# Layer 0's softmax totals in 256 columns, one inverse per head and query, spread by transfers between partitions, and a gate by tanh

## The chip, the cores and the metric

The kernel runs on one core of a Trainium2 chip. The metric is the device time of the launch in microseconds. All data are float32.

## The reference, cut to what matters

Two layers run over x of shape (1, 128, 256, 256): S = 128 rows, each with 256 positions and 256 channels. Both are "x + attention(group norm of x)". Layer 0, which the change touches, has 8 heads of 32 channels:

```python
bias = jnp.einsum('nijz,zh->nhij', pair_repr, bias_proj)[:, None]
gate = jax.nn.sigmoid(msa_repr @ gate_proj).reshape(bs, s, r, head, c)
q, k, v = jnp.split(msa_repr @ qkv_proj, 3, axis=-1)
...
sim = jnp.einsum('nsqhc,nskhc->nshqk', q, k) * scale
sim = jax.nn.softmax(sim, axis=-1)
sim = sim + bias
attend = jnp.einsum('nshqk,nskhc->nsqhc', sim, v) * gate
out = attend.reshape(bs, s, r, cm) @ out_proj
```

The bias is added after the softmax. With E = exp(scale q k) unnormalised and z its sum over the keys, the attended values are (E v) / z + bias v, times the gate. Layer 1 is an attention with 4 heads of 64 channels in a band of 16 positions; the change leaves its arithmetic alone.

## The kernel before, in words

First `pair_repr` is projected to the bias tile `bias_sb`, and x is read once for its statistics. Then layer 0 runs over the 128 rows. A row's data lie with channels on the 128 partitions, in two halves: a tile [128, 2, 256] is (channel within the half, half, query). Heads 0 to 3 are in half 0, heads 4 to 7 in half 1; head 4 x half + j has partitions 32j to 32j + 31, which the code calls `strip(j)`.

The order of the instructions of PE (TensorE), ACT (ScalarE) and DVE (VectorE) is the order written in the code: the loop stands in a block `manual_schedule` for these three. For SP (SyncE, the queue of DMAs) and POOL (GpSimd) a scheduler chooses the order. [...]

One step s of the loop "for s in range(S)" works on several rows at once:

- `scores(s, half)` makes the scores of four heads (16 products into four PSUM banks, line 794) and their exponentials `ex` (L807). It gives back a function that issues the fourth of them. The PSUM banks for scores and projections are one ring of five.
- `join_tiles(s, half, j)` adds the two key halves of two heads (L816), which gives `both`.
- `sum_heads(s - 1)` makes on PE the totals `zs` (L840) and the bias part `bv` (L826). In `zs` the stationary tile is 32 columns of ones, so that each total appears on all 32 partitions of its head.
- `divide(s - 1)` copies `zs` to `z` on ACT (L853), makes d = (1 + e) z (L855), where e = exp(-gate), and inverts it (L856).
- `attend(s - 1)` makes `av`, E v, on PE, and then on DVE at = (bv z + av) d (L871, L872, L874).
- `stretch(names, i, s - 1)` makes the projections q and k, or v and g, of a pair of rows two steps ahead, by seven products in place of eight (`Seven`, `two_of_them`), and among its last products the output projection `po` of row s - 1, which reads `at` (L577 is the line of all these products). `po` comes in four parts, each after one of the last products.
- `least(s - 1)` keeps the minimum of z for a check at the end (L861), `normal(s + 4)` transposes and normalises a later row (L539, L775) and starts the load of x two rows on (L357), and `finish(s - 1)` adds the residual (L885), takes statistics for layer 1 (L889), and every second row stores to the DRAM tensor `x1` (L891).

After the loop come the last row, the statistics of layer 1 and layer 1 itself, whose rows are loaded as `yg` (L750). Layer 1 already spreads inverses by DMA: `by_transfer` sends four rows of `rz` to DRAM (`rz_far`, L1162) and reads them back broadcast (`near`, L1166).

Of the kernel before, what the change touches and what calls it, by code (L numbers as in the profile page):

```python
# [9 lines left out]
F32 = mybir.dt.float32  # L10
# [5 lines left out]
P = 128  # L16
# [23 lines left out]
def conv_preact_kernel(  # L40
# [97 lines left out]
    for base, per_row, per_group in ((0, 1, -CG), (CG - 1, -1, CG)):  # L138
        nc.gpsimd.affine_select(
            out=within.rearrange("p (g c) -> p g c", c=CG), in_=within.rearrange("p (g c) -> p g c", c=CG),  # L140
            compare_op=ALU.is_ge, fill=0.0, base=base, pattern=[[per_group, P // CG], [0, CG]],
            channel_multiplier=per_row,
        )

    w_out_t = const.tile([P, 2, C], F32, name="w_out_t")
# [215 lines left out]
    with ExitStack() as early:  # L361
# [10 lines left out]
        def load_weights():  # L372
            w_raw = pr_pool.tile([P, 8, C], F32, tag="pr", name="w_raw")
            nc.gpsimd.dma_start(out=w_raw[:, 6:8, :], in_=out_w.rearrange("(t p) c -> p t c", p=P))
            nc.gpsimd.dma_start(out=w_raw[:, 0:6, :], in_=w_in.rearrange("(t p) c -> p t c", p=P))
            nc.gpsimd.dma_start(out=w_nat[:, 6:8, :], in_=w_out.rearrange("(t p) c -> p t c", p=P))
            nc.gpsimd.dma_start(out=b_raw[0:6], in_=b_in.rearrange("(t p) -> t p", p=P))
            nc.gpsimd.dma_start(
                out=b_raw[6:8].rearrange("h (a r) -> h a r", a=A),
                in_=b_out.rearrange("(a h r) -> h a r", a=A, h=2),  # L380
            )
            for h in range(2):
                cols = slice(h * P, (h + 1) * P)
                for to, t0, t1 in ((out_sb, 6, 8), (w_nat, 0, 6)):
                    nc.gpsimd.tensor_copy(
                        to[:, 0 : t1 - t0, cols].rearrange("p t (a r) -> p t a r", a=A),
                        w_raw[:, t0:t1, :].rearrange("p t (a h r) -> p t h a r", a=A, h=2)[:, :, h],
                    )

        def turn_weights():  # L390
            for o4 in range(2):
# [340 lines left out]
    with ExitStack() as both:  # L732
# [3 lines left out]
        quarters1 = {w: Quarters(st1, w_in_t, n * C, f"1{w}") for n, w in enumerate("qk")}  # L736
        quarters1["o"] = Quarters(st1, w_out_t, 0, "1o")
        big1 = both.enter_context(tc.tile_pool(name="big1", bufs=2))
        ygs = {}
        rz_far = dram.tile([2, 2, 4, R], F32, name="rz_far")  # L740

        def load1(g):
            if g * XG < S and g not in ygs:

                if g % 7 < 2:
                    yg = big.tile([P, XG * (R // B), C // A], F32, tag="xg", name=f"yg{g}")
                    yg = yg.rearrange("p n c -> p (n c)").rearrange("p (s h q) -> p s h q", h=2, q=R)
                else:
                    yg = big1.tile([P, XG, 2, R], F32, tag="yg", name=f"yg{g}", bufs=5)
                nc.sync.dma_start(out=yg, in_=rows(x1, g * XG, XG))  # L750
                ygs[g] = yg

        with ExitStack() as lay0:
# [58 lines left out]
            def join_tiles(s, half, j):  # L812

                if s < S:
                    ex, both = hd[s, half]
                    nc.vector.tensor_tensor(both[:, j : j + 2], ex[:, j : j + 2, 0, :], ex[:, j : j + 2, 1, :], ALU.add)  # L816
# [15 lines left out]
            def sum_heads(s):  # L832
                if s < 0:
                    return
                zs = ps_av.tile([P, 2, R], F32, tag="z", name=f"zs{s}")
                bv0 = ps_av.tile([P, 2, R], F32, tag="bv", name=f"bv{s}")
                for half in range(2):
                    both = hd[s, half][1]
                    for j in range(4):
                        nc.tensor.matmul(  # L840
                            zs[D0 * j : D0 * (j + 1), half, :], lhsT=ones[:, 0:D0], rhs=both[:, j, :],
                            start=True, stop=True,
                        )
                products(bv0, s, lambda h, kt: bias_sb[:, kt, h, :])
                hd[s] = bv0
                return zs

            def divide(s, zs):
                if s < 0:
                    return  # L850
                i, r = divmod(s, 2)
                z = att.tile([P, 2, R], F32, tag="z", name=f"z{s}", bufs=1)
                nc.scalar.activation(z, zs, AF.Identity, accum_out=zsum[:, s : s + 1])  # L853
                d = att.tile([P, 2, R], F32, tag="d", name=f"d{s}", bufs=1)
                nc.vector.scalar_tensor_tensor(d, res["g", i][:, 2 * r : 2 * r + 2, :], 1.0, z, op0=ALU.add, op1=ALU.mult)  # L855
                nc.vector.reciprocal(d, d)  # L856
                hd[s, "z"] = (z, d)

            def least(s, z):
                if s >= 0:  # L860
                    nc.vector.tensor_reduce(zmin[:, s : s + 1], z, axis=AX.XY, op=ALU.min)  # L861

            def attend(s):
                if s < 0:
                    return
                (ex0, _), (ex1, _), bv0 = hd.pop((s, 0)), hd.pop((s, 1)), hd.pop(s)
                av = ps_av.tile([P, 2, R], F32, tag="av", name=f"av{s}")
                products(av, s, lambda h, kt: (ex0, ex1)[h // 4][:, h % 4, kt, :])
                z, d = hd.pop((s, "z"))
                t = att.tile([P, 2, R], F32, tag="t", name=f"t{s}", bufs=1)  # L870
                nc.vector.tensor_tensor(t, bv0, z, ALU.mult)  # L871
                nc.vector.tensor_tensor(t, av, t, ALU.add)  # L872
                at = row.tile([P, 2, R], F32, tag="at", name=f"at{s}", bufs=1)
                nc.vector.tensor_tensor(at, t, d, ALU.mult)  # L874
                st[s]["at"] = at

            def finish(s):
# [35 lines left out]
            with tc.manual_schedule(engines={mybir.EngineType.PE, mybir.EngineType.Activation, mybir.EngineType.DVE}):  # L913
# [7 lines left out]
                sum_rows(1)  # L921
                most1 = Most(st1, stats1, 3, 1)
                for s in range(S):
                    scores(s, 0)()
                    zs = sum_heads(s - 1)
                    join_tiles(s, 0, 0)
                    divide(s - 1, zs)
                    if s % 2 == 0:
                        e = res["g", s // 2]
                        nc.scalar.activation(e, e, AF.Exp, scale=-1.0)  # L930
                    z = hd[s - 1, "z"][0] if s > 0 else None
                    rest = ((0, 2), (1, 0), (1, 2))
                    if s < S - 1:
                        attend(s - 1)
                        last_exp = scores(s, 1)
                        if s == 4:
                            for weights in quarters1.values():
                                weights.sum()
                        stretch(("qk", "vg")[s % 2], s // 2 + 1, s - 1, last_exp)
                        for half, j in rest:  # L940
                            join_tiles(s, half, j)
                        least(s - 1, z)
                        if s >= S - 3:
                            most1.join(s - S + 3)
                        normal(s + 4)
                        if s % 2 == 1:
                            sum_rows((s + 3) // 2)
                        finish(s - 1)
                    else:

                        scores(s, 1)()
                        for half, j in rest:
                            join_tiles(s, half, j)
                        least(s - 1, z)
                        attend(s - 1)
                load1(0)
                load1(1)
                warm = proj_bank("warm")
# [6 lines left out]
                divide(S - 1, sum_heads(S - 1))  # L965
                last_z = hd[S - 1, "z"][0]
                attend(S - 1)
                for s in (S - 2, S - 1):
                    if s == S - 1:
                        keep_on(4)  # L970
                    for _ in one_by_one(out_sb, st[s]["at"], f"po{s}", lambda ps: st[s].update(po=ps), B):
                        pass
                    finish(s)
# [6 lines left out]

        with ExitStack() as lay:
            ps_av = psum(lay, "1", 4, 0)
            row = lay.enter_context(tc.tile_pool(name="row1", bufs=4))
            att = lay.enter_context(tc.tile_pool(name="att1", bufs=2))
            st, hd, outs = {s: {} for s in range(S)}, {}, {}
# [366 lines left out]
    with tc.If(sure < P):  # L1352
        with ExitStack() as lay:
# [69 lines left out]
            def again(layer, s, mean, rstd):  # L1423
# [38 lines left out]
                if layer == 0:  # L1462
                    ps = by_channel(gate_sb, 0, xn, "pg2")
                    e = two.tile([P, 2, R], F32, tag="e2", name="e2")
                    nc.scalar.activation(e, ps, AF.Exp, scale=-1.0)
                    nc.vector.tensor_scalar(e, e, 1.0, None, op0=ALU.add)
                    nc.vector.reciprocal(e, e)
                    nc.vector.tensor_tensor(at, at, e, ALU.mult)
                po = by_channel(out_sb if layer == 0 else w_out_t, 0, at, f"po2_{layer}")
                o = two.tile([P, 2, R], F32, tag="o2", name=f"o2_{layer}")  # L1470
                if layer == 0:
# [61 lines left out]
```

## Time and profile before

| | |
|---|---|
| median of 3 runs | 3150.04 us (3149.86 to 3153.88) |
| profiled execution | 3153.9 us, span 3152.1 us |
| mean granted TensorE clock | 0.993 |
| share of the span on the chain that ended last | PE 91%, DMA 5%, DVE 2%, ACT 1% |
| layer 0, rows | about 206 to 2045 us |
| one row's step in layer 0 | 14.5 us on average |

The span is the time from the first to the last instruction on the core; what the profiled execution took beyond it lies before and after. "Busy" is the time in which an engine has an instruction under way. Matmuls are pipelined, and their ends are modelled, so PE's busy time is an upper reading. PEld is the load of the stationary tile, which runs beside the products. SPq is SP issuing a DMA, not the transfer itself. In a row of the timeline "[0.87 <-ACT ex L807]" is the idle time before the instruction and what ended it.

### The profile page before, as it was taken

To read this page: it belongs to the slowest core of one execution; us is meant where nothing else is said; L and a number is where in the kernel's file an instruction comes from. 1 tells how busy PE (TensorE), PEld (TensorE's weight loads), DVE (VectorE), ACT (ScalarE), POOL (GpSimd) and SP (SyncE) were. 2 spreads that over 40 slices of the span, in tenths; PEclk is the share of its full clock that TensorE was granted. 3 is DMA by queue.
4 is the path that set the end of the run, shared out by engine and by line. 5 is a ranking of instruction groups with operands and counts; after the bars stand their busy time and mean duration, and the time that the engine had idled before them with its cause. 6 is when DMAs were issued, how large, how long until landed. Compare 5 with 4: busy or idle time off the path is not lost.

```text
span 3152.1 us, 128861 instructions
## 1 busy us (share of the span) xinstructions
PE 3075.5 (98%) x57467; PEld 2114.1 (67%) x57467; DVE 2544.5 (81%) x4140; ACT 1870.0 (59%) x4064; POOL 1622.5 (51%) x1651
## 2 busy tenths in 40 slices
PE   6889999999999999999999999999999999999997
PEld 4556666666666666665666666568888888888886
DVE  4669999999999999999999999956666666666665
ACT  4666666666666666666666666645555555555553
POOL 3034444444444444444444544357777777776774
PEclk9989999999999999999999999999999999999999
DMA  9941111111111111111111111114444444444443
GB/s 374 424 121 43 43 43 36 43 36 43 36 39 40 40 40 36 43 36 43 36 42 37 36 43 36 36 35 98 93 103 96 102 96 97 103 99 100 93 99 70
DMA packets 357266, 245.08 MB, mean 78 GB/s; under 512 B 276072, under 2 KB 342112, under 8 KB 350560
## 3 DMA queue, kind: packets, MB, share of 16 engines
q1 hardware_dynamic: 355808, 234.39, 27.3%
q8 instruction: 453, 7.42, 1.0%
q0 software_dynamic: 752, 2.36, 0.2%
q14 instruction: 109, 0.89, 0.1%
q10 hardware_dynamic: 144, 0.00, 0.0%
HBM read 169.09 MB, written 67.62 MB: 75 GB/s over the span
## 4 chain that ended last, share of the span: by engine, by line
PE 91%; DMA 5%; DVE 2%; ACT 1%; issue 0%; POOL 0%; SPq 0%; DVEq 0%; POOLq 0%; ACTq 0%
PE sim L794 8%; PE po L577 7%; PE p1v L1055 7%; PE bv L826 7%; PE av L826 7%; PE p1q L577 6%; PE p1o L577 6%; PE pv L577 6%; PE pq L577 6%; PE p1k L577 6%; PE pk L577 5%; PE pg L577 5%; DMA pr<-in_L_conv_pair_repr_dram 4%; PE zs L840 4%; PE 1sim L1076 3%; PE 1av L1117 3%
## 5 line engine op out<-in xcount | busy, mean ns | idle before, releaser
L807 ACT ACTIVATE ex<-sim 128x512 f32<-128x512 f32 x1024 | 547.6, 605 | 422.2 <-PE sim L794 422.2
L816 DVE TENSOR_TENSOR both<-ex 128x512 f32<-128x512 f32 x512 | 487.8, 991 | 71.2 <-ACT ex L807 71.0
L856 DVE RECIPROCAL d<-d 128x512 f32<-128x512 f32 x128 | 429.2, 3353 | 4.4
L618 POOL TENSOR_TENSOR v<-v,twovg 128x256 f32<-128x256 f32 x64 | 78.3, 1223 | 544.4 <-ACT twovg L637 544.4
L577 PE MATMUL po<-at,out_sb 128*32 128x256 f32 x4096 | 291.5, 380 | 4.1 <-DVE at L874 4.1
L794 PE MATMUL sim<-q,k 32*64 32x256 f32 x8192 | 288.4, 387 | 1.2 <-ACT ex L807 1.2
L826 PE MATMUL bv<-bias_sb,v 128*32 128x256 f32 x4096 | 244.5, 379 | 0.7 <-DVE t L871 0.7
L826 PE MATMUL av<-ex,v 128*32 128x256 f32 x4096 | 244.5, 379 | 0.0
L1086 POOL TENSOR_TENSOR 1p<-1ex,seen 128x768 f32<-128x768 f32 x127 | 231.0, 1819 | 13.9 <-ACT 1ex L1084 13.9
L1055 PE MATMUL p1v<-w_in_t,1xn 128*64 128x128 f32 x4096 | 237.7, 274 | 0.3 <-POOL place L990 0.3
L794 PEld LDWEIGHTS sim<-q,k 32*64 32x64 f32 x8192 | 152.1, 131 | 126.9 <-issue 79.3
L1055 PEld LDWEIGHTS p1v<-w_in_t,1xn 128*64 128x64 f32 x4096 | 222.3, 137 | 21.5 <-PE p1k L577 20.2
L677 ACT ACTIVATE 1q<-p1q,bqk 128x256 f32<-128x256 f32 x192 | 91.1, 474 | 244.1 <-PE p1q L577 244.1
L1186 DVE TENSOR_TENSOR 1at<-1av,1near 128x512 f32<-128x512 f32 x128 | 82.5, 686 | 151.5 <-DMA 1near<-rz_far 129.0
L618 POOL TENSOR_TENSOR q<-q,twoqk 128x256 f32<-128x256 f32 x64 | 52.0, 812 | 292.4 <-ACT twoqk L637 292.4
L826 PEld LDWEIGHTS bv<-bias_sb,v 128*32 128x32 f32 x4096 | 133.2, 110 | 88.7 <-issue 1.1
L826 PEld LDWEIGHTS av<-ex,v 128*32 128x32 f32 x4096 | 133.2, 110 | 87.9 <-issue 0.4
L577 PEld LDWEIGHTS po<-at,out_sb 128*32 128x32 f32 x4096 | 131.0, 110 | 70.9 <-issue 4.5
L1093 POOL TENSOR_TENSOR 1zp<-1p 128x512 f32<-128x512 f32 x127 | 161.9, 1275 | 10.0
L568 POOL TENSOR_TENSOR 1ts<-1xn 128x256 f32<-128x256 f32 x64 | 47.0, 734 | 232.9 <-ACT 1xn L1016 232.9
L775 DVE TENSOR_SCALAR xn<-xt,mean,rstd 128x256 f32<-128x256 f32 x256 | 160.4, 666 | 0.0
L1062 ACT COPY 1v<-p1v 128x512 f32<-128x512 f32 x128 | 75.1, 587 | 135.1 <-PE p1v L1055 131.7
(300 smaller groups left out, 7687.6 us busy)
## 6 DMA issues: line engine op xcount, KB each, us to landing
pr<-in_L_conv_pair_repr_dram SPq DMA_DIRECT2D x32, 1024.0 KB
xs<-in_x_dram SPq DMA_DIRECT2D x16, 2048.0 KB
x<-o SPq DMA_DIRECT2D x64, 512.0 KB
yg<-x SPq DMA_DIRECT2D x64, 512.0 KB
out_dram<-1o SPq DMA_DIRECT2D x256, 128.0 KB
xg<-in_x_dram SPq DMA_DIRECT2D x252, 128.0 KB
1near<-rz_far SPq DMA_DIRECT2D x124, 256.0 KB
rz_far<-1rz SPq DMA_DIRECT2D x124, 4.0 KB
```

The source lines that it names most:

```text
L577: nc.tensor.matmul(out[cols], lhsT=lhsT[:, cols], rhs=rhs, **flags)
L618: nc.gpsimd.tensor_tensor(self.to[:, 0], self.to[:, 0], two, ALU.add)
L775: nc.vector.tensor_scalar(xns[i][:, 2 * r + half, :], xt[:, half, :], mean0[:, half : half + 1], rstd0[:, half : half + 1], op0=ALU.subtra ...
L794: nc.tensor.matmul(sims[j][KB * c : KB * (c + 1), kt, :], lhsT=k[p0 : p0 + D0, 2 * r + half, k0 : k0 + KB], rhs=q[p0 : p0 + D0, 2 * r + ha ...
L807: nc.scalar.activation(ex[:, j], sims[j], AF.Exp, scale=1.0 / math.sqrt(D0))
L816: nc.vector.tensor_tensor(both[:, j : j + 2], ex[:, j : j + 2, 0, :], ex[:, j : j + 2, 1, :], ALU.add)
L826: nc.tensor.matmul(to[D0 * j : D0 * (j + 1), half, :], lhsT=v[:, 2 * r + half, c0 : c0 + D0], rhs=weights(4 * half + j, kt), start=(kt == ...
L840: nc.tensor.matmul(zs[D0 * j : D0 * (j + 1), half, :], lhsT=ones[:, 0:D0], rhs=both[:, j, :], start=True, stop=True,)
L856: nc.vector.reciprocal(d, d)
L1055: nc.tensor.matmul(ps[KB * half : KB * (half + 1), b, :], lhsT=xns[i][:, 2 * r + kt, KB * b : KB * (b + 1)], rhs=w_in_t[:, kt, 2 * C + P * ...
L1086: engine.tensor_tensor(p.rearrange("p j (r c) -> p (j r) c", c=WROW)[:, :, 0 : 2 * WSTEP] .rearrange("p r (t c) -> p r t c", c=WSTEP)[:, : ...
L1093: engine.tensor_tensor(zp, p[:, :, 0:R], p[:, :, R : 2 * R], ALU.add)
```

## The change

In layer 0, each head's total now stands on one partition instead of 32. The stationary tile `place0` has ones in 16 columns, 0 to 15 for half 0 and 16 to 31 for half 1, so the totals of both halves fill one tile [128, 256]: partitions 32j to 32j + 15 hold head j, the next 16 hold head 4 + j. `z` and its inverse `rz` have 256 columns instead of 512. Eight DMAs a row, issued from SP, each copy one partition of `rz` to the 32 partitions of its head and half in `near`. For the last row two products with the tile `spread0` and a copy on ACT do this. The products with `v` are then at = (av near + bv)(1 + tanh(gate/2)), in the new function `gated`; the factor one half of the sigmoid is put into `out_sb`. On ACT the fourth exponential of `scores(s, 0)` comes after the copy of `z`. On DVE the order of a step becomes: first join, inverse, second join, minimum, normalisation of row s + 4, the three operations of `gated`, the two joins of half 1, residual. The pool of the `yg` tiles is opened in layer 1 instead of ahead of layer 0. The code that recomputes a row in another way when a total is out of range gets the factor 2 that undoes the half.

```diff
+    place0 = const.tile([P, 2, B], F32, name="place0")
+    nc.gpsimd.memset(place0, 0.0)
+    for half in range(2):
+        nc.gpsimd.memset(place0[:, half, 16 * half : 16 * (half + 1)], 1.0)
+    spread0 = const.tile([P, 2, P], F32, name="spread0")
+    for half in range(2):
+        nc.gpsimd.tensor_copy(
+            spread0[:, half].rearrange("p (j d) -> p j d", d=D0),
+            ident[:, 16 * half :: B].unsqueeze(2).to_broadcast([P, A, D0]),
...
+                    if t0 == 6:
+                        nc.gpsimd.tensor_scalar(to, raw, 0.5, None, op0=ALU.mult)
...
-                    yg = big1.tile([P, XG, 2, R], F32, tag="yg", name=f"yg{g}", bufs=5)
+                    yg = pools["yg"].tile([P, XG, 2, R], F32, tag="yg", name=f"yg{g}", bufs=5)
...
                         nc.tensor.matmul(
-                            zs[D0 * j : D0 * (j + 1), half, :], lhsT=ones[:, 0:D0], rhs=both[:, j, :],
-                            start=True, stop=True,
+                            zs[strip(j), 0, :], lhsT=place0[:, half, :], rhs=both[:, j, :],
+                            start=(half == 0), stop=(half == 1),
                         )
...
             def divide(s, zs):
...
-                z = att.tile([P, 2, R], F32, tag="z", name=f"z{s}", bufs=1)
-                nc.scalar.activation(z, zs, AF.Identity, accum_out=zsum[:, s : s + 1])
-                d = att.tile([P, 2, R], F32, tag="d", name=f"d{s}", bufs=1)
-                nc.vector.scalar_tensor_tensor(d, res["g", i][:, 2 * r : 2 * r + 2, :], 1.0, z, op0=ALU.add, op1=ALU.mult)
-                nc.vector.reciprocal(d, d)
-                hd[s, "z"] = (z, d)
+                z = att.tile([P, R], F32, tag="z", name=f"z{s}", bufs=1)
+                nc.scalar.activation(z, zs[:, 0, :], AF.Identity, accum_out=zsum[:, s : s + 1])
+                rz = att.tile([P, R], F32, tag="rz", name=f"rz{s}")
+                nc.vector.reciprocal(rz, z)
+                near = att.tile([P, 2, R], F32, tag="near", name=f"near{s}")
+                if s < S - 1:
+                    for j in range(A):
+                        for half in range(2):
+                            p = B * j + 16 * half
+                            nc.sync.dma_start(
+                                out=near[strip(j), half, :],
+                                in_=rz[p : p + 1].unsqueeze(1).to_broadcast([1, B, R]),
+                            )
+                else:
+                    ps = proj_bank(f"near{s}")
+                    for half in range(2):
+                        nc.tensor.matmul(ps[:, half, :], lhsT=spread0[:, half], rhs=rz, start=True, stop=True)
+                    nc.scalar.copy(near, ps)
+                hd[s, "z"] = (z, near)
...
-                z, d = hd.pop((s, "z"))
+                hd[s, "av"] = (av, bv0)
+
+            def gated(s):
...
                 t = att.tile([P, 2, R], F32, tag="t", name=f"t{s}", bufs=1)
-                nc.vector.tensor_tensor(t, bv0, z, ALU.mult)
-                nc.vector.tensor_tensor(t, av, t, ALU.add)
+                nc.vector.tensor_tensor(t, av, near, ALU.mult)
+                nc.vector.tensor_tensor(t, bv0, t, ALU.add)
                 at = row.tile([P, 2, R], F32, tag="at", name=f"at{s}", bufs=1)
-                nc.vector.tensor_tensor(at, t, d, ALU.mult)
+                nc.vector.scalar_tensor_tensor(
+                    at, res["g", i][:, 2 * r : 2 * r + 2, :], 1.0, t, op0=ALU.add, op1=ALU.mult
+                )
...
                 for s in range(S):
-                    scores(s, 0)()
+                    last_exp = scores(s, 0)
                     zs = sum_heads(s - 1)
                     join_tiles(s, 0, 0)
                     divide(s - 1, zs)
+                    last_exp()
                     if s % 2 == 0:
                         e = res["g", s // 2]
-                        nc.scalar.activation(e, e, AF.Exp, scale=-1.0)
...
+                        nc.scalar.activation(e, e, AF.Tanh, scale=0.5)
+                    attend(s - 1)
+                    join_tiles(s, 0, 2)
+                    if s > 0:
+                        least(s - 1, hd[s - 1, "z"][0])
+                    normal(s + 4)
+                    gated(s - 1)
+                    last_exp = scores(s, 1)
                     if s < S - 1:
-                        attend(s - 1)
-                        last_exp = scores(s, 1)
...
                         stretch(("qk", "vg")[s % 2], s // 2 + 1, s - 1, last_exp)
-                        for half, j in rest:
-                            join_tiles(s, half, j)
-                        least(s - 1, z)
+                    else:
+                        last_exp()
+                    for j in (0, 2):
+                        join_tiles(s, 1, j)
+                    if s < S - 1:
...
-                        normal(s + 4)
...
                         finish(s - 1)
-                    else:
-
-                        scores(s, 1)()
-                        for half, j in rest:
-                            join_tiles(s, half, j)
-                        least(s - 1, z)
-                        attend(s - 1)
...
                 attend(S - 1)
+                gated(S - 1)
```

More of the change, by code (lines that the diff above doesn't have):

```diff
@@ L384, in load_weights @@
                 for to, t0, t1 in ((out_sb, 6, 8), (w_nat, 0, 6)):
[L385 to L388, printed above, removed]
+                    to = to[:, 0 : t1 - t0, cols].rearrange("p t (a r) -> p t a r", a=A)
+                    raw = w_raw[:, t0:t1, :].rearrange("p t (a h r) -> p t h a r", a=A, h=2)[:, :, h]
+                    if t0 == 6:
+                        nc.gpsimd.tensor_scalar(to, raw, 0.5, None, op0=ALU.mult)
+                    else:
+                        nc.gpsimd.tensor_copy(to, raw)
         def turn_weights():
@@ L738, in conv_preact_kernel @@
         big1 = both.enter_context(tc.tile_pool(name="big1", bufs=2))
-        ygs = {}
+        ygs, pools = {}, {}
         rz_far = dram.tile([2, 2, 4, R], F32, name="rz_far")
@@ L850, in divide @@
                     return
-                i, r = divmod(s, 2)
-                z = att.tile([P, 2, R], F32, tag="z", name=f"z{s}", bufs=1)
-                nc.scalar.activation(z, zs, AF.Identity, accum_out=zsum[:, s : s + 1])
-                d = att.tile([P, 2, R], F32, tag="d", name=f"d{s}", bufs=1)
-                nc.vector.scalar_tensor_tensor(d, res["g", i][:, 2 * r : 2 * r + 2, :], 1.0, z, op0=ALU.add, op1=ALU.mult)
-                nc.vector.reciprocal(d, d)
-                hd[s, "z"] = (z, d)
+                z = att.tile([P, R], F32, tag="z", name=f"z{s}", bufs=1)
[17 more added lines that the diff above has]
+                hd[s, "z"] = (z, near)
             def least(s, z):
                 if s >= 0:
-                    nc.vector.tensor_reduce(zmin[:, s : s + 1], z, axis=AX.XY, op=ALU.min)
+                    nc.vector.tensor_reduce(zmin[:, s : s + 1], z, axis=AX.X, op=ALU.min)
             def attend(s):
@@ L868, in attend @@
                 products(av, s, lambda h, kt: (ex0, ex1)[h // 4][:, h % 4, kt, :])
-                z, d = hd.pop((s, "z"))
+                hd[s, "av"] = (av, bv0)
+            def gated(s):
+                if s < 0:
+                    return
+                (av, bv0), near = hd.pop((s, "av")), hd.pop((s, "z"))[1]
+                i, r = divmod(s, 2)
                 t = att.tile([P, 2, R], F32, tag="t", name=f"t{s}", bufs=1)
-                nc.vector.tensor_tensor(t, bv0, z, ALU.mult)
-                nc.vector.tensor_tensor(t, av, t, ALU.add)
+                nc.vector.tensor_tensor(t, av, near, ALU.mult)
+                nc.vector.tensor_tensor(t, bv0, t, ALU.add)
                 at = row.tile([P, 2, R], F32, tag="at", name=f"at{s}", bufs=1)
-                nc.vector.tensor_tensor(at, t, d, ALU.mult)
+                nc.vector.scalar_tensor_tensor(
+                    at, res["g", i][:, 2 * r : 2 * r + 2, :], 1.0, t, op0=ALU.add, op1=ALU.mult
+                )
                 st[s]["at"] = at
@@ L927, in conv_preact_kernel @@
                     divide(s - 1, zs)
+                    last_exp()
                     if s % 2 == 0:
                         e = res["g", s // 2]
-                        nc.scalar.activation(e, e, AF.Exp, scale=-1.0)
-                    z = hd[s - 1, "z"][0] if s > 0 else None
-                    rest = ((0, 2), (1, 0), (1, 2))
+                        nc.scalar.activation(e, e, AF.Tanh, scale=0.5)
[6 more added lines that the diff above has]
+                    last_exp = scores(s, 1)
                     if s < S - 1:
-                        attend(s - 1)
-                        last_exp = scores(s, 1)
                         if s == 4:
@@ L939, in conv_preact_kernel @@
                         stretch(("qk", "vg")[s % 2], s // 2 + 1, s - 1, last_exp)
-                        for half, j in rest:
-                            join_tiles(s, half, j)
-                        least(s - 1, z)
+                    else:
+                        last_exp()
+                    for j in (0, 2):
+                        join_tiles(s, 1, j)
+                    if s < S - 1:
                         if s >= S - 3:
                             most1.join(s - S + 3)
-                        normal(s + 4)
                         if s % 2 == 1:
@@ L982, in conv_preact_kernel @@
             ps_av = psum(lay, "1", 4, 0)
+            pools["yg"] = lay.enter_context(tc.tile_pool(name="yg1", bufs=1))
             row = lay.enter_context(tc.tile_pool(name="row1", bufs=4))
@@ L1467, in again @@
                     nc.vector.reciprocal(e, e)
-                    nc.vector.tensor_tensor(at, at, e, ALU.mult)
+                    nc.vector.scalar_tensor_tensor(at, at, 2.0, e, op0=ALU.mult, op1=ALU.mult)
                 po = by_channel(out_sb if layer == 0 else w_out_t, 0, at, f"po2_{layer}")
```

## The prediction

> **What bounds the kernel now.** I first took the busy shares of the page, then the table of busy time by stretch, then who waited for whom on PE.
>
> ```profile
> PE 3075.5 (98%) x57467; PEld 2114.1 (67%) x57467; DVE 2544.5 (81%) x4140; ACT 1870.0 (59%) x4064; POOL 1622.5 (51%) x1651
> ```
>
> In the stretch from 300 to 1900 us, which is layer 0 in its steady state, PE has no gap at all. The columns are length, then busy time (count) of PE, PEld, DVE, ACT and POOL, then the clock, the DMA share and GB/s:
>
> ```profile
> 300.00:1900.00 1600.00, 1600.00 (x34916) 977.48 (x34912) 1500.56 (x1771) 1033.91 (x2156) 727.29 (x664) 1.00 0.15 40
> PE po L577 <- DVE at L874: 4.1, 2, 3.6
> ```
>
> The second line is PE's wait for `at`, the tile that the change recomputes: 4.1 us in two instances over the span. So DVE, 94% busy there, is not waited for, and time freed on it is worth almost nothing. What counts is whether the new path to `at` is longer than PE can hide.
>
> One row's step, from the timeline (start, length, engine, line, operation). I call 1013.99, the first scores of the row, T. The next row's scores start at 1028.45, so a step is 14.46 us.
>
> ```profile
> 1013.99 1.12 PE L794 MATMUL sim<-q,k 32*64 32x256 f32 x32
> 1015.04 1.07 PE L840 MATMUL zs<-both,ones 128*32 128x256 f32 x16
> 1025.10 0.35 PEld L577 LDWEIGHTS po<-at,out_sb 128*32 128x32 f32 x8
> 1015.17 2.07 ACT L807 ACTIVATE ex<-sim 128x512 f32<-128x512 f32 x4 [1.32 <-PE sim L794]
> 1017.09 0.63 ACT L853 ACTIVATE z<-zs 128x512 f32<-128x512 f32 x1
> 1024.27 0.37 ACT L611 COPY midq<-pq 128x256 f32<-128x256 f32 x1
> 1016.29 1.06 DVE L816 TENSOR_TENSOR both<-ex 128x512 f32<-128x512 f32 x1 [0.87 <-ACT ex L807]
> 1017.91 1.13 DVE L855 SCALAR_TENSOR_TENSOR d<-g,z 128x512 f32<-128x512 f32 x1 [0.56 <-ACT z L853]
> 1019.07 3.35 DVE L856 RECIPROCAL d<-d 128x512 f32<-128x512 f32 x1
> 1022.34 0.63 DVE L871 TENSOR_TENSOR t<-bv,z 128x512 f32<-128x512 f32 x1
> 1023.79 0.69 DVE L874 TENSOR_TENSOR at<-t,d 128x512 f32<-128x512 f32 x1
> ```
>
> PE needs `at` at T+11.1 (1025.10); it has it at T+10.5 (1024.48). The margin is 0.6 us, and everything after `at` on PE, 3.4 us of the step, stands behind that load.
>
> For transfers I looked at SyncE's issues, in layer 0 (first row) and in layer 1, where a similar spreading exists:
>
> ```profile
> 1042.99 1.90 SPq L357 DMA_DIRECT2D xg<-in_x_dram  x4
> 2316.04 1.09 SPq L1162 DMA_DIRECT2D rz_far<-1rz  x2
> 2317.67 1.12 SPq L1166 DMA_DIRECT2D 1near<-rz_far  x2
> ```
>
> One issue occupies SP for about 0.53 us whether it moves 4 KB or 128 KB (1.09/2; the four take 0.31 and then three times 0.53). SP was free again at 2317.13 and waited for the first `rz_far` to land before 2317.67, so a small transfer lands about 1.6 us after its issue starts.
>
> [...] The trace has tables loaded only at layer borders; tanh itself it does not show.
>
> **The change, part by part**, per row unless said.
>
> *PE.* The eight `zs` products keep shape and count, only their target shrinks: 0. *ACT.* `z` is 256 wide instead of 512: 0.37 instead of 0.63. The fourth exp of the first half moves behind `z`; its bank is wanted again by the first projection, at T+6.5, so 0. The gate's tanh takes the place of an exp of 1.06 us: 0. If each gate did switch tables, that would be up to 2 x 1.28 us (the load at 2052.88) every second row on ACT, which is 65% busy; I take 0.
>
> *DVE.* Gone: `d` (909 ns mean), half of the reciprocal (1.68), half of the minimum (about 0.3), together 2.9 us. No time is gained, as PE does not wait for DVE. Least and the normalisation of row s+4 (0.76 + 1.3) move ahead of the gate, under the transfer. The latter has its input two rows early.
>
> *SP.* New: eight issues for each of 127 rows. Behind them in the queue stand, every second row, the four `xg` loads, 4 us later than now but needed two rows on: 0. Ahead of them stands the store of two rows of `x`, which waits for the residual at about T+0.7 to 2.2, issues in 0.40 us, and is off the DMA engines some 3 us after that (the table of 0.75 us slices shows no bytes by then). `near` starts later: 0.
>
> *The path to `at`* is the price:
> - three exps from T+1.2, so `z` starts at T+2.6; 0.37 for it, 0.2 until DVE may read it (now 0.82 from its start to L855's, for 0.63): T+3.2;
> - the reciprocal, behind the first join (done by T+3.0 to 3.4), 1.68: T+4.9;
> - eight issues: the last starts 0.35 + 6 x 0.53 later, T+8.45;
> - landing, 1.6 for a small one: T+10.05;
> - each transfer reads one partition's 1 KB 32 times[...]: T+11.25;
> - [...]three operations, 0.73 + 0.73 (start to start now) + 0.9 (two SBUF inputs, as `d`): `at` at T+13.7.
>
> PE wants it at T+11.1: **2.6 us of idle PE** in each of the 126 steps that hold a `po`. DVE has finished the normalisation by T+8.6 and stands waiting; behind it are the joins of the second half (2 us), done by T+15.7, before the next `zs` at T+18.1. Nothing else becomes late. 126 x 2.6 = 328 us.
>
> *Border.* In the last step the joins of the second half now stand behind row 126's gate. PE resumed `zs` at 2049.72, 9.0 us after that row's scores; now about T+15.7, 6.7 later. The last row's own path is shorter (reciprocal 1.68 less, `d` gone, a product and a copy added): about 2.5 back. Net +4. The `yg` buffers that move to layer 1 are first read after its first stretch: 0. GpSimd's set-up lies in the first 200 us, where it is busy for 35: 0.
>
> Sum against the profiled execution (3153.9 us, span 3152.1): 3153.9 + 328 + 4 = 3486; it was 0.12% above the median of 3150.0, so 3482 for the median.
>
> **The rivals.**
> - [...]Reads of one partition run as fast as others, `near` lands at T+10.05, `at` at T+12.5, idle 1.4 us: 126 x 1.4 + 4 = 180, so 3330. [...]Against: `xg`, into 32 partitions, moves at 156 to 203 GB/s while the store from 128 moved at 350.
> - *Transfers one behind another.* [...]landing at T+15.9, `at` at T+18.3, idle 7.2: 3150 + 910 + 4 = 4064. In-between values are possible.
> - *Hidden, no slower.* If the eighth lands by T+8.6, where DVE ends the normalisation, `at` is there at T+11.0 and PE never waits. It takes issues of at most 0.32 us[...]: 3154, no change. The first issue after a pause takes 0.31, but those behind it 0.48 and a gap.
> - *Faster.* PE would have to be waiting for DVE now; 4.1 us at most is there to be won.
>
> **How the numbers follow.** A 2.6 us stall (2.0 to 3.3): 0.42. [...]: 0.28. Queued transfers (3.3 to 7.3): 0.20. Hidden: 0.07. Faster: 0.03. The likeliest gives 3482. The range 3290 to 3780 runs from a stall of 1.1 to 5.0 us, leaving out the hidden and faster cases and half of the queued one. Some 0.2% (6 us) is what a measurement can tell from no change; of the hidden case part would lie above it: faster 0.03, same 0.05, slower 0.92.
>
> **What would show it.** In the changed profile: `po` waiting for `at` some 126 times at 1 to 3 us; PE's share in layer 0 at about 85%; DVE waiting for DMA `near` before the product of `av`; eight SP issues of about 0.5 us directly after the reciprocal; a step of about 17 us. A step of 14.5 us would refute all of it; a wait at `z`, the fourth exp or `zs` instead of `po` would show a path that I costed at nothing.

## The result, and the profile after

The changed kernel takes 3829.52 us (median of 4 runs, 3818.09 to 3837.51) against 3150.76 us: 1.2145 times the time before, with an interval of 1.2124 to 1.2166. The direction was forecast, the size was not: 679 us were lost where the prediction had 332, and the time lies above the stated range. The profiled execution has a span of 3829.2 us.

First the page's busy times (same columns as before), and the layer 0 stretch of the table of busy time, which was 1.00 in PE's clock column and 0.15 in DMA share before:

```profile
PE 3259.5 (85%) x57471; PEld 2227.2 (58%) x57471; DVE 2017.7 (53%) x4012; ACT 1836.2 (48%) x4065; POOL 1487.2 (39%) x1656
```

```profile
300.00:2000.00 1700.00, 1366.95 (x26985) 836.98 (x26981) 804.49 (x1280) 777.90 (x1668) 467.69 (x514) 0.93 0.31 42
```

DVE lost 527 us of work, as intended. PE now stands still for a fifth of layer 0, and yet its busy time over the span rose by 184 us with the same products: its clock was at 0.93 on average there. The two tables of waits (total, times, longest) say for what PE and DVE waited:

```profile
PE po L590 <- DVE at L905: 487.0, 126, 8.2
PE zs L853 <- DVE both L829: 8.7, 1, 8.7
DVE t L902 <- DMA near<-rz: 494.2, 86, 7.9
DVE t L902 <- DMA xg<-in_x_dram: 252.0, 41, 7.1
```

The first line was 4.1 us in 2 instances before; now each of the 126 steps has its wait. The two DVE lines are one wait, 127 times for `near`: `xg` stands in 41 rows only because it was the last transfer to land there; the gate doesn't read it.

One row in the timeline, beginning with the first scores; T is now 1010.48:

```profile
1010.48 1.12 PE L807 MATMUL sim<-q,k 32*64 32x256 f32 x32
1013.11 0.40 ACT L865 ACTIVATE z<-zs 128x256 f32<-128x256 f32 x1
1013.63 1.75 DVE L867 RECIPROCAL rz<-z 128x256 f32<-128x256 f32 x1 [0.16 <-ACT z L865]
1015.41 5.57 SPq L873 DMA_DIRECT2D near<-rz  x8
1016.85 0.70 DVE L788 TENSOR_SCALAR xn<-xt,mean,rstd 128x256 f32<-128x256 f32 x2
1023.36 0.69 DVE L902 TENSOR_TENSOR t<-av,near 128x512 f32<-128x512 f32 x1 [5.81 <-DMA xg<-in_x_dram]
1024.88 0.69 DVE L905 SCALAR_TENSOR_TENSOR at<-g,t 128x512 f32<-128x512 f32 x1
1025.72 0.71 PE L590 MATMUL po<-at,out_sb 128*32 128x256 f32 x8 [3.70 <-DVE at L905]
1026.15 1.13 PE L590 MATMUL pg<-ts,sums_g 128*32 128x256 f32 x8
1026.98 1.16 PE L590 MATMUL pv<-qkv_sb,ts 128*32 128x128 f32 x16
1027.83 1.16 PE L590 MATMUL po<-at,out_sb 128*32 128x256 f32 x8
1030.57 1.12 PE L807 MATMUL sim<-q,k 32*64 32x256 f32 x32
```

The path is the predicted one: reciprocal done at T+4.9, eight issues on SP, DVE idle from 1017.55 to 1023.36, `at` at T+15.1, PE idle for 3.70 us. The new thing stands behind it. The groups at 1026.15, 1026.98, 1027.83 begin 0.83 to 0.85 us apart. In the kernel before they did so 0.43 us apart:

```profile
1025.32 0.61 PE L577 MATMUL po<-at,out_sb 128*32 128x256 f32 x8
1025.75 0.61 PE L577 MATMUL pk<-ts,sums_k 128*32 128x256 f32 x8
```

After this stall PE runs at half rate: its granted clock is 0.50 from 1026.17 to 1029.58, 3.41 us.

Over rows 3 to 124 of both traces, a step has gone from 14.48 to 19.81 us: 4.0 us more between the product ahead of `po` and `po`, and 1.33 us more from `po` to the scores of the next row's second half (9.97 instead of 8.64). 126 x 5.34 = 673, and 7.3 more at the border's `zs`: 680, against 677 between the two spans.

### The profile page after: what moved, and what is told of

It is laid out like the page before. It is cut to its first block, busy times and chain, and to the rows that moved or that the text cites. A ratio compares the mean times of both kernels' runs of the same rounds, so it can differ in the third digit from the quotient of the medians.

```text
span 3829.2 us, 130233 instructions
## 1 busy us (share of the span) xinstructions
PE 3259.5 (85%) x57471; PEld 2227.2 (58%) x57471; DVE 2017.7 (53%) x4012; ACT 1836.2 (48%) x4065; POOL 1487.2 (39%) x1656
## 3 DMA queue, kind: packets, MB, share of 16 engines
q0 software_dynamic: 752, 2.36, 0.2%
## 4 chain that ended last, share of the span: by engine, by line
PE 50%; DVE 16%; SPq 15%; DMA 13%; issue 3%; ACT 2%; POOL 0%; DVEq 0%; ACTq 0%; POOLq 0%
SPq L873 15%; PE po L590 8%; DMA near<-rz 7%; PE p1v L1088 6%; DVE rz L867 6%; PE p1q L590 5%; PE p1o L590 5%; PE p1k L590 5%; PE sim L807 4%; PE zs L853 3%; PE 1sim L1109 2%; DVE at L905 2%; DMA pr<-in_L_conv_pair_repr_dram 2%; DVE t L903 2%; DVE t L902 2%
## 5 line engine op out<-in xcount | busy, mean ns | idle before, releaser
L590 PE MATMUL po<-at,out_sb 128*32 128x256 f32 x4096 | 385.4, 468 | 487.0 <-DVE at L905 487.0
L590 PEld LDWEIGHTS po<-at,out_sb 128*32 128x32 f32 x4096 | 180.7, 135 | 602.0 <-issue 577.6
L902 DVE TENSOR_TENSOR t<-av,near 128x512 f32<-128x512 f32 x128 | 88.4, 691 | 750.3 <-DMA near<-rz 494.2
L829 DVE TENSOR_TENSOR both<-ex 128x512 f32<-128x512 f32 x512 | 362.7, 729 | 120.4 <-ACT ex L820 118.9
L918 DVE TENSOR_TENSOR o<-po,xt 128x512 f32<-128x512 f32 x128 | 88.6, 692 | 442.5 <-PE po L590 442.5
L631 POOL TENSOR_TENSOR v<-v,twovg 128x256 f32<-128x256 f32 x64 | 46.8, 731 | 567.9 <-ACT twovg L650 567.9
L634 POOL TENSOR_TENSOR v<-v,midv 128x512 f32<-128x512 f32 x64 | 81.6, 1274 | 416.9 <-ACT v L628 416.9
L634 POOL TENSOR_TENSOR q<-q,midq 128x512 f32<-128x512 f32 x64 | 81.6, 1275 | 401.7 <-ACT q L628 401.7
L867 DVE RECIPROCAL rz<-z 128x256 f32<-128x256 f32 x128 | 223.8, 1748 | 13.7 <-ACT z L865 13.2
L626 ACT COPY midg<-pg 128x256 f32<-128x256 f32 x64 | 23.8, 373 | 309.3 <-PE pg L590 309.3
```

The source lines that it names most:

```text
L590: nc.tensor.matmul(out[cols], lhsT=lhsT[:, cols], rhs=rhs, **flags)
L634: nc.gpsimd.tensor_tensor(self.to[:, 2:4], self.to[:, 2:4], self.mid, ALU.add)
L867: nc.vector.reciprocal(rz, z)
L902: nc.vector.tensor_tensor(t, av, near, ALU.mult)
```

## The experiments

Each was timed beside the kernel before on the same chip: e1 to e4 on one, e5 to e8 on a second, e9 on a third. On these three the kernel before took 3150.8, 3150.8 and 3150.3 us. The table gives, from each profile, the mean time from the reciprocal's end to DVE's product of `av` and `near`, PE's whole wait for `at`, and the step.

| kernel | us | reciprocal to `near` in use, us | PE waits for `at`, us | step, us |
|---|---|---|---|---|
| before | 3150.8 | none | 4.1 | 14.48 |
| changed | 3829.5 | 7.99 | 487.0 | 19.81 |
| e1, 32 source partitions | 3665.3 | 7.35 | 397.6 | 18.49 |
| e2, `near` of the row before | 3155.1 | not waited for | 5.6 | 14.48 |
| e3, filler of 4 | 3673.8 | 7.97 | 217.5 | 18.55 |
| e8, filler of 7 | 3641.8 | 7.98 | 54.6 | 18.29 |
| e4, by product | 3289.7 | no transfer | 3.4 | 15.54 |
| e5, four transfers | 3363.5 | 5.66 | 176.8 | 16.09 |
| e6, through DRAM | 3467.9 | 6.12 | 243.1 | 16.94 |
| e7, two queues | 3460.7 | 6.32 | 141.0 | 16.90 |
| e9, two queues, other order | 3384.4 | 5.66 | 66.8 | 16.30 |

**Is the wait all of it? e2.**

```diff
-                near = att.tile([P, 2, R], F32, tag="near", name=f"near{s}")
+                near = att.tile([P, 2, R], F32, tag="near", name=f"near{s}", bufs=3)
...
+                nears[s] = near
+                near = nears[s - 1] if 0 < s < S - 1 else near
```

> The changed kernel, but the gate of a row multiplies with the near of the row before, which landed a step ago: every transfer is still made, none is waited for in its own step. It leaves out the right inverse for rows 1 to 126. Theory that the wait for near is the whole loss: PE waits for at no more, a step of 14.5 us, 3155 to 3160 us (the border costs up to 7). Rival, that the new order, the tanh, the smaller tiles or the DMA traffic cost something of themselves: a step above 14.5 us, 3200 us or more.

Measured: 3155.07 us, ratio 1.0012 (1.0005 to 1.0019). From its page and its waits:

```profile
PE 3075.1 (97%) x57471; PEld 2113.2 (67%) x57471; DVE 1985.3 (63%) x4012; ACT 1841.1 (58%) x4065; POOL 1497.1 (47%) x1656
PE po L590 <- DVE at L907: 5.6, 2, 4.2
```

All transfers are made, the order, the tanh and the smaller tiles are in, and the step is back at 14.48 us. So none of them costs anything that shows: the loss is the wait, with what it does to PE. It also shows what the relief of DVE is worth here. DVE has 559 us less to do than in the kernel before, and nothing is won.

**Why is PE slow after the wait? e3 and e8.** Products of no use go into the bank that `po` then overwrites, ahead of its first part:

```diff
+        for _ in range(fill):
+            nc.tensor.matmul(ps[:, 0, :], lhsT=ident, rhs=out_sb[:, 0, :], start=True, stop=True)
```

> The changed kernel, with four products of no use (1.7 us of PE) ahead of the first part of po, into the bank that po then overwrites. Theory that PE's clock falls to half[...]: the idle stretch shrinks from 4.0 to 2.3 us, the products after it run at full rate (8.64 us from po to the next half's scores instead of 9.97), and 126 x 1.33 = 168 us are won although PE does more: 3660 us. Rival, that PE is slow there for another reason (operands, PSUM, power): the products stay slow, 3830 us; if the filler delays po: up to 4040 us.

> As the filler of four products, with seven (3.0 us): PE's idle stretch is about 1.0 us. Theory that the filler only keeps the clock up and the wait stays: the rest of the slow products goes (8.93 to 8.64 us after po), 126 x 0.29 = 37 us less than with four: 3640 us. Rival, that the filler itself delays po: more than with four, 3700 us or above.

Measured: 3673.75 us with four, 3641.82 us with seven (ratios 1.1651, 1.1598 to 1.1703, and 1.156, 1.1541 to 1.158). Work was added and 156 and 188 us were won. The layer 0 stretch, e3 and then e8 (PE's clock is the third figure from the end):

```profile
300.00:2000.00 1700.00, 1542.64 (x29512) 942.78 (x29508) 847.40 (x1369) 831.65 (x1777) 506.77 (x550) 0.98 0.33 45
```

```profile
300.00:2000.00 1700.00, 1662.31 (x30651) 1054.31 (x30647) 857.19 (x1394) 848.97 (x1812) 517.53 (x560) 1.00 0.34 46
```

The clock goes from 0.93 through 0.98 to 1.00, and the time from `po` to the next half's scores from 9.97 through 8.93 to 8.67 us (8.64 before). The step of e8 is 3.8 us longer than before, about the bare wait.

In the changed kernel, between 300 and 2000 us, the granted clock falls to half 68 times, 65 times for 3.41 us and three times for 6.83, and all these stretches begin on one grid of 3.41 us. What tells a wait with slow products after it from one without is how its idle time lies in the windows of this grid. Here are the wait of the row before the one above, and windows of the grid around the two waits (PE's busy time is the second figure):

```profile
1007.33 0.64 PE L590 MATMUL po<-at,out_sb 128*32 128x256 f32 x8 [3.57 <-DVE at L905]
1002.27:1005.69 3.42, 1.48 (x28) 0.65 (x20) 0.65 (x1) 1.29 (x4) 1.42 (x2) 1.00 0.32 26
1005.69:1009.10 3.41, 1.77 (x36) 1.30 (x40) 2.62 (x5) 0.59 (x2) 0.00 (x0) 1.00 0.00 0
1022.75:1026.17 3.42, 0.45 (x9) 0.36 (x13) 2.67 (x5) 0.00 (x0) 0.00 (x0) 1.00 0.78 140
1026.17:1029.58 3.41, 3.41 (x45) 2.48 (x41) 0.61 (x2) 0.96 (x2) 0.74 (x1) 0.50 0.02 5
```

The wait of 3.57 us falls into two windows, with PE idle for 1.94 and 1.64 us, and nothing slow follows. The wait of 3.70 us has 2.97 us in one window, and the next window is at half clock. Each of the 68 stretches follows a window in which PE was idle for 2.11 us or more, and no such window at full clock goes without (idle by the trace's modelled ends); of the windows at full clock that were followed by full clock, the longest idle one had 2.07 us. In the three stretches of 6.83 us the second half follows a window at half clock with 0.90 to 1.12 us of idle PE. So a wait may or may not cost clock: of the changed kernel's waits for `at`, half clock was granted within the next 3.41 us after 13 of the 26 below 3.5 us (2.88 the shortest), 48 of the 62 from 3.5 to 4 us, and all 38 above.

**What makes the wait 8 us long? e1 and e5.** In e1 only the source is another. The first of the two forecasts below is that of the single source partition being the limit:

```diff
-                                in_=rz[p : p + 1].unsqueeze(1).to_broadcast([1, B, R]),
+                                in_=rz[strip(j)],
```

> The changed kernel, but each of the eight transfers reads the 32 partitions of its strip, 1 KB each, instead of one partition 32 times: the same number of issues and bytes[...]. It leaves out the right placing (half of the channels get the inverse of another head). [...]1 KB packets take well under 100 ns instead of about 240, an issue 0.53 us instead of 0.67, the last landing comes 1.6 us after its issue instead of 3.3; at lies at about T+12.4, PE idles 1.4 us a step[...]: about 3330 us. Issue theory (SP's issue and landing cost what they cost for a transfer of this size, whatever the source): 3830 us, as the changed kernel.

Measured: 3665.32 us, ratio 1.1634 (1.1614 to 1.1653). Neither forecast had it right. SP's queue and the layer 0 stretch of e1:

```profile
970.24 5.32 SPq L873 DMA_DIRECT2D near<-rz  x8
```

```profile
300.00:2000.00 1700.00, 1408.39 (x28756) 865.26 (x28748) 849.90 (x1365) 830.01 (x1777) 503.07 (x550) 0.96 0.18 45
```

With about as many bytes a microsecond, the DMA engines are busy 0.18 of the time instead of 0.31: a packet of 1 KB takes 62 ns on average instead of 239. So the first forecast is right that the source holds the packets. Whether it is the one source partition, or the same 1 KB being read 32 times, e1 doesn't tell, as it changes both. But the issues stayed where they were, 4.82 us from the reciprocal to the start of the last, 4.71 in the changed kernel. The source only sets how long after the last issue `near` is there: 3.0 us in the changed kernel, 2.1 in e1 (rows with no transfer of 16 KB in flight behind the last issue, see the end).

In e5 four transfers are left out:

```diff
-                        for half in range(2):
...
+                            in_=rz[B * j : B * j + 1].unsqueeze(1).to_broadcast([1, B, R]),
...
+                near = near[:, 0:1, :].to_broadcast([P, 2, R]) if s < S - 1 else near
```

> The changed kernel with four transfers a row instead of eight: half 0's only, and the gate uses them for both halves (left out: the inverses of heads 4 to 7 in rows 0 to 126). Theory that the number of issues, about 0.66 us each, sets the landing: the last issue starts 1.9 us after the reciprocal instead of 4.7, at lies at T+12.2, PE idles about 1.1 us a step, its clock stays up: about 3295 us. Rival, [...]the same here, so this run only measures the price of an issue: 2.7 to 2.8 us less stall for four of them, and 1.3 us less for the clock.

Measured: 3363.45 us, ratio 1.0671 (1.0654 to 1.0689). The last issue starts at 1.97 us, as expected, but `near` is in use 3.7 us after it and not 3.0. The packets took 304 ns instead of 239. The four sources, partitions 0, 32, 64 and 96, follow each other without the others in between, and order matters in e9 below; that this is the reason here was not shown. Four issues fewer give 2.3 us.

**Can the path be shortened? e6, e7, e9.** In e6 the rows go through DRAM, in e7 half of the transfers are issued by ACT, and e9 changes the order of e7's transfers alone:

```diff
+                    far = rz_far0[s % 2]
+                    nc.sync.dma_start(out=far, in_=rz.rearrange("(n c) q -> n c q", c=16)[:, 0, :])
+                    for j in range(A):
+                        nc.sync.dma_start(
+                            out=near[strip(j)].rearrange("p h q -> p (h q)"),
+                            in_=far[2 * j : 2 * j + 2].rearrange("n q -> (n q)").partition_broadcast(B),
...
```

```diff
+                    def send(half, queue):
...
+                            queue.dma_start(
...
+                    send(0, nc.sync)
+                    hd[s, "send"] = lambda: send(1, nc.scalar)
...
+                    if s > 0:
+                        hd.pop((s - 1, "send"))()
                     attend(s - 1)
```

```diff
-                        for j in range(A):
+                        for j in ((0, 2, 1, 3), (2, 0, 3, 1))[half]:
```

> The changed kernel, but the inverse goes through DRAM, as layer 1's does: one write of eight rows, then four broadcast reads, five issues in place of eight and no single-partition source. Theory of issues: write landed 2.1 us after the reciprocal, the last read issued 1.6 to 1.9 us later, landed 2.6 us after that: near 6.5 us after the reciprocal instead of 8.0, PE idles about 2.4 us, no clock loss: 3460 us. Rival, that the second hop costs as much as the three issues saved: 8 us again, 3830 us.

> The changed kernel with half 1's four transfers issued from ACT's queue, behind the tanh, half 0's from SP. Theory that SP's issuing is the limit: both queues have issued by 2.0 us after the reciprocal, landing at 5.1, at T+12.3, idle 1.2 us: 3310 us, plus up to 60 us where ACT's exponentials come 0.8 us late. Rival, [...]landing at 7.0, idle 2.9 us: 3530 to 3600 us.

> The kernel with two queues, with the order of the transfers changed alone: SP sends partitions 0, 64, 32, 96, ACT 80, 16, 112, 48 (before: 0, 32, 64, 96 and 16, 48, 80, 112). [...] the last packet ends some 1.0 us sooner after the reciprocal (4.5 instead of 5.5), DVE starts the gate at 5.3 instead of 6.3, PE's wait for at falls from 1.4 to about 0.4 us: 3335 to 3350 us. Rival, [...]no change, 3461 us.

Measured: e6 3467.89 us (1.1012, 1.0986 to 1.1038), e7 3460.74 us (1.098, 1.0962 to 1.0998), e9 3384.41 us (1.0741, 1.0723 to 1.0759). In e6 a second hop is cheaper than three more issues and the slow source: 6.12 us instead of 7.99. In e7 both queues have started their last issue 2.28 us after the reciprocal, and the last packet still ends at 5.49. In e9 the same issues at the same times, in another order, have it end at 4.88 us, with packets of 159 ns instead of 195, and the time falls by 76 us. Only the sequence of the transfers differs between the two, so this shows their order to matter; by what mechanism was not shown. Each transfer has its target strip with its source, so the order of targets changed too. In e1 the targets follow each other as in the changed kernel and the packets take 62 ns, so targets alone don't explain the 239; their part in e9 was not measured apart. The gain is 0.66 us a row, where 1.0 was expected. What ACT's issuing costs stands in PE's waits, e7 and then e9:

```profile
PE po L590 <- DVE at L908: 141.0, 125, 6.6
PE pk L590 <- ACT ex L820: 57.3, 62, 2.0
PE pg L590 <- ACT ex L820: 56.7, 63, 1.8
```

```profile
PE po L590 <- DVE at L908: 66.8, 125, 5.9
PE pg L590 <- ACT ex L820: 57.0, 63, 2.0
PE pk L590 <- ACT ex L820: 56.5, 62, 1.8
```

114 us of new wait, since the exponentials of the second half stand behind the four issues on ACT (2.79 us for the four in e7's row at 1000.18, and the exponentials start at 1003.01).

**Without transfers, e4.**

```diff
+                def by_product():
+                    ps = proj_bank(f"near{s}")
+                    for half in range(2):
+                        nc.tensor.matmul(ps[:, half, :], lhsT=spread0[:, half], rhs=rz, start=True, stop=True)
+                    nc.scalar.copy(near, ps)
...
-                    gated(s - 1)
                     last_exp = scores(s, 1)
+                    if s > 0:
+                        hd[s - 1, "spread"]()
+                    gated(s - 1)
```

> The changed kernel, but every row's inverse is spread by two products with spread0 and a copy on ACT behind the scores of the second half, as the last row's is, and no transfer is made. Theory that the transfers are the loss: near is there at T+8.9, at at T+11.1, hidden; PE has two more products of 0.43 us a row: 126 x 0.86 = 108, so about 3260 us. Rival, that the rest of the change (order, tanh) also costs: 3300 us or more.

Measured: 3289.66 us, ratio 1.044 (1.0422 to 1.0457). PE no longer waits for `at`; the step is longer by PE's own work:

```profile
1000.24 1.13 PE L873 MATMUL near<-rz,spread 128*128 128x256 f32 x4
1001.30 0.64 PE L590 MATMUL pv<-qkv_sb,xn 128*32 128x128 f32 x16
```

The two products take 1.06 us to the next, not 0.86: 0.2 us on top for each row, some 25 of the 30 us by which the expectation was low. Of the variants that leave nothing out this is the fastest, and it loses to the kernel before, which gets each total onto 32 partitions at no cost: its stationary tile of ones has 32 columns, as `place0` has, and the 16 matmul records of a row's `zs` take 1.07 us in both kernels.

## Why the prediction was right and wrong

Right: the bound (PE, with no wait for DVE), so that freed DVE time would give nothing (e2); the place of the loss, `po` waiting for `at` in 126 steps; what was costed at nothing outside the path, order and other queues included (e2: all of them together, with the border, 4 us); the tanh, which takes 1.08 us where the exp took 1.06, with no table loaded between 206 and 2734 us; the path in its order; the border's `zs`, 7.3 us more against 6.7.

Wrong are terms of the sum for `at`, and one that was missing:

| step of the path | predicted, us | measured, us |
|---|---|---|
| reciprocal ends | T+4.9 | T+4.9 |
| first to last issue | 3.53 | 4.68 |
| last issue to DVE's first operation | 2.9 | 3.28 |
| the gate's three operations | 2.36 | 2.18 |
| `at` | T+13.7 | T+15.1 |
| PE's wait for `at`, mean | 2.6 | 3.87 |
| slow products after it | 0 | 1.33 |

The step that failed first is "eight issues": 0.53 us each was taken from transfers between SBUF and DRAM. Transfers within SBUF took 0.55 for the first interval and 0.65 to 0.74 on average for the rest. These averages hold two things. The usual interval is 0.63 us, and 81 issues in rows 3 to 124 took 0.8 to 1.6 us; each of these overlapped a 16 KB transfer of an instruction queue, which 113 of the other 895 did. No run took those transfers away, so this cause is not shown. e1 shows that neither the broadcast nor the single source makes the 0.63. e6's reads from DRAM came every 0.55 us. Why an issue within SBUF is dearer was not found.

In "landing" two errors nearly cancel. For reading one partition it counts 1.2 us (T+10.05 to T+11.25), which was the author's estimate and shown by no trace of before; e1 gives 0.9. The 1.6 us for a small transfer were too little: in e1 it is 2.1. The 3.28 of the table is over their sum: it is the mean of 3.05 us in rows with no 16 KB transfer in flight behind the last issue and 3.51 in the other half of the rows.

Third, PE's clock does not occur in the sum, and so was costed at nothing without a reason. That would have been too little at 2.6 us already: in e6, with 243.1 us of waits in 126 steps, 1.9 us each, the products after the wait lost 0.37 us a step (9.01 us from `po` to the next half's scores). At 3.9 us they lose 1.33 us a step, 168 us in all. A stall error of 1.3 us became 2.7 us a step.

Of the rivals, that reads of one partition run as fast as others is refuted by e1 (62 ns a packet against 239). "Transfers one behind another" did not happen: the last packet of the eight ended 7.3 us after the reciprocal, not 11 (T+15.9). "Hidden" and "faster" are out.

## What to carry to other kernels

Here the short transfers cost the issuing queue more than the DMA engines: a row's eight held SP for 5.3 us, while their 256 packets come to 3.8 us of each of the 16 engines at 239 ns, and to 1.0 us in e1 at 62 ns. So count issues, and count them at the price of a transfer of the same kind of source and target (0.63 us within SBUF here, where 0.53 was taken from transfers to and from DRAM). Where the engine that bounds the kernel waits for the result, a path of many small transfers is bought from that engine's time, whatever it frees elsewhere. And when a wait of PE is worked out, look whether it comes near those after which the clock fell here: with waits of 1.4 us on average (e5) the clock in layer 0 was 1.00, with 1.9 (e6) 0.98, with 3.9 (the changed kernel) 0.93. The products after the wait can then be slow too, in the changed kernel more often the longer it was, and filling the gap with products of no use won that part back (e8, 188 us).

## What the runs showed of the hardware that was not expected

- In the changed kernel 2.11 us or more of idle PE within one window of 3.41 us at full clock was followed by half clock in the next window (68 of 68), and 2.07 us or less never was.
- An issue from SP for a transfer within SBUF (32 KB) usually follows the one before after 0.63 us in a row of eight, 0.65 to 0.74 on average; ACT's, in e7, after 0.75 on average.
- 1 KB packets out of one partition took 239 ns on average in the changed kernel, out of 32 partitions 62 ns (e1). Another order of the transfers out of single partitions was worth 0.66 us of the landing (e7 and e9).
- Transfers of 16 KB on an instruction queue (about 1.1 us each) run beside the kernel's own. In e1, rows with one of them in flight behind the last issue had `near` about 1 us later than rows without (3.1 to 3.2 us against 2.1 after the last issue); in the changed kernel 0.3 to 0.6 us later. This is a comparison within a trace; no run took those transfers away.
